# A gated cross-attention and ternary FFN block on one core: weights in column quarters rounded in two steps, TensorE fillers, quantised activations turned by DMA, and new step lists

## The chip, the core and the metric

The kernel runs on one core of a Trainium2 chip. A core has five engines that run their own instruction streams in order: TensorE (PE in the profile, with its weight loads shown apart as PEld), VectorE (DVE), ScalarE (ACT), GpSimd (POOL) and SyncE (SP, which here only issues DMAs). They meet through semaphores. The metric is the device time of one execution in microseconds (us). Three runs of the kernel before took 536.57, 537.95 and 539.39 us; the median is 537.95 us.

## What is computed

The block works on 16 batches of 128 tokens with 512 features. Cut to what matters:

```python
# attention: 32 query heads, 8 key/value heads, head size 16, keys = values = ctx
x = x + tanh(g_xattn) * attention(layernorm(x), ctx, ctx)

# FFN, 512 -> 2048 -> 512
def act_quant(x):                # one scale per token
    s = 127 / clip(max|x|, 1e-5);  return clip(round(x * s), -128, 127) / s
def weight_quant(w):             # one scale per matrix, values -1, 0, 1
    s = clip(mean|w|, 1e-5);       return clip(round(w / s), -1, 1) * s
def h_bitlinear(x, w):
    return act_quant(hadamard(x)) @ weight_quant(w).T
h = silu(h_bitlinear(n, w_gate)) * h_bitlinear(n, w_up)      # n = layernorm(x)
x = x + tanh(g_ffn) * h_bitlinear(h, w_down)
```

## The kernel before, in words

**Steps and lists.** The body is a set of small functions, each a step for one batch `b` (and a part of it). Three lists written out by hand give the order: `PROLOGUE` once, `PLAN` nine times (i = 2 to 10, a step with offset d works on batch i + d), `EPILOGUE` once. `InOrder` (lines 23 to 42) pins each engine's instructions to that order, so the lists are the order of every engine's queue, SP's among them. Every instruction is recorded at line 34, its call; so the profile is read by tile names.

**Attention of one batch.** `normed` takes layer-norm statistics of x (DVE), a power on POOL for 1/sqrt, and applies them (DVE, tile `q`). `q_transposed` turns q on PE (`tpq`), ACT copies it (`qT`). `scores` multiplies with the keys (`sc`, fp32, 32 rows of the array at a time) and DVE takes each row's maximum (`mx`). `split_max` on POOL splits the maxima into three bf16 parts, `max_transposed` turns them (`tpm`, `mT`). `weights` makes the scores the other way round less the maxima (`sT`), ACT takes exp (`ex`); `summed` multiplies with the values (`av`, `avT`); `residual` turns the result back (`tpo`), divides it (DVE, `ga`) and POOL adds it to x.

**FFN of one batch.** `in_norm`: statistics (`stf`, `mvf`, `vef` on DVE, `rstdf` on POOL), DVE applies them (`hn`), POOL does two of the Hadamard steps (`hb`). `in_hadamard` turns that on PE and multiplies with a 128x128 Hadamard matrix (`z`). `in_quant` on DVE: maximum, scale, integers `qe` (int16), and the factors `dq`. `in_transposed` turns qe by four PE transposes (`tpe`) and ACT casts the result to bf16 (`qTe`). `gate_up(b, n)` makes 512 columns of both products (`gu`, bf16, 8 matmuls), `gated` takes Silu on ACT (`sg`) and multiplies on DVE (`h`). `hidden_transposed` turns h (`tpf`, ACT copy `hT`), `hadamard` multiplies (`y`, ACT copy into `za`), `butterfly` does three of the four remaining Hadamard steps on DVE (`zb`, `za`), `magnitudes` takes absolute values on ACT, `out_quant` in three parts finds the maximum (`junk`, `amax_f`) and writes the integers `qf` (int16). `out_transposed` turns each half of qf by eight PE transposes (`tpf<-ident,qf`) and an ACT cast (`qTf`); `out_down` multiplies with w_down (`yo`) and DVE adds x (`res`), which SP sends out.

**Weights, in the prologue.** Each matrix comes as four row quarters of 1 MB (`wst_gate`, `wst_up`, `wst_down`). `mag_*` sums absolute values on ACT, `mean_*` gives the scale. A quarter is then rounded in one of two ways: `rounded_*`, three passes on POOL (multiply and add a large constant, clamp, subtract it), or `compared_*`, two compares on DVE. Two quarters of gate and up go each way; down's four quarters all go to POOL. A row quarter holds all 2048 columns of one chunk of the contraction, so the first `gate_up` needs all four quarters of both matrices.

**Buffers around the change.** Staged weights and the tiles `za` and `zb` share six buffers (`big`). `ps_x` has four PSUM tiles, shared by all transposes and small products, `ps_s` two larger ones for `sc`, `sT` and `gu`. `qf` and `qTf` have one buffer each.

Of the kernel before, what the change touches and what calls it, by code (L numbers as in the profile page):

```python
# [12 lines left out]
I16 = mybir.dt.int16  # L13
AX = mybir.AxisListType
# [4 lines left out]

MAGIC = 12582912.0  # L20
# [25 lines left out]
def flamingo_kernel(  # L46
# [6 lines left out]
    g_attn: bass.AP,  # L53
    g_ffn: bass.AP,
# [3 lines left out]
    h128: bass.AP,  # L58
# [27 lines left out]
    def load_pair(b: int):  # L86
# [14 lines left out]
    load_pair(0)  # L101
    sel_f = w1.tile([P, 2, P], F32, tag="hbT", name="sel_f")
    nc.sync.dma_start(sel_f, sel)
    gates = const.tile([P, 2], F32, name="gates")
    nc.sync.dma_start(gates[:, 0:1], g_attn.partition_broadcast(P))
    nc.sync.dma_start(gates[:, 1:2], g_ffn.partition_broadcast(P))
# [10 lines left out]
    had = const.tile([P, P], F32, name="had")  # L117
    tanh_g = const.tile([P, 2], F32, name="tanh_g")

    wq = {  # L120
        "gate": const.tile([P, KC, FF], BF16, name="wq_gate"),
        "up": const.tile([P, KC, FF], BF16, name="wq_up"),
        "down": const.tile([P, FC, E], BF16, name="wq_down"),
    }
    wsc = const.tile([P, 3], F32, name="wsc")
# [12 lines left out]
    def layer_norm(b: int, kind: str, dst, src):  # L138

        st = tiny.tile([P, 6], F32, tag="st", name=f"st{kind}_{b}")  # L140
        nc.vector.bn_stats(st, xs[b])
        mv = tiny.tile([P, 2], F32, tag="mv", name=f"mv{kind}_{b}")
        nc.vector.bn_aggr(mv, st)
        rstd = tiny.tile([P, 1], F32, tag="rstd", name=f"rstd{kind}_{b}")
        ve = tiny.tile([P, 1], F32, tag="ve", name=f"ve{kind}_{b}")
        nc.vector.tensor_scalar(ve, mv[:, 1:2], EPS, None, ALU.add)
        nc.gpsimd.tensor_tensor(rstd, ve, mhalf, ALU.pow)
        nc.vector.tensor_scalar(dst, src, mv[:, 0:1], rstd, ALU.subtract, ALU.mult)
# [9 lines left out]
    qTs, mTs, exs, avs, maxima = {}, {}, {}, {}, {}  # L158

# [140 lines left out]
    def weight_steps(name: str, src: bass.AP, i: int):  # L300
        NQ = 4
        shape = wq[name].shape
        q = shape[1] // NQ
# [3 lines left out]
        half = const.tile([P, 2], F32, name=f"half_{name}")  # L307
        part = lambda c: wq[name][:, c * q : (c + 1) * q, :]

        def load(c: int):  # L310
            st[c] = big.tile([P, q, shape[2]], F32, tag="big", name=f"wst_{name}_{c}")
            nc.sync.dma_start(
                st[c], src.rearrange("(c p) f -> p c f", p=P)[:, c * q : (c + 1) * q, :]
            )

        def mag(c: int):

            nc.scalar.activation(part(c), st[c], AF.Abs, accum_out=asum[:, c : c + 1])

        def mean():  # L320
            tot = ps_x.tile([P, NQ], F32, tag="x", name=f"tot_{name}")
            nc.tensor.matmul(tot, lhsT=ones, rhs=asum, start=True, stop=True)
            m = tiny.tile([P, 1], F32, tag="mean", name=f"mean_{name}")
            nc.vector.tensor_reduce(m, tot, AX.X, ALU.add)
            nc.vector.tensor_scalar(m, m, 1.0 / NW, EPS, ALU.mult, ALU.max)
            nc.vector.reciprocal(inv, m)
            nc.vector.tensor_scalar(half[:, 0:1], m, 0.5, None, ALU.mult)
            nc.vector.tensor_scalar(half[:, 1:2], m, -0.5, None, ALU.mult)
            nc.vector.tensor_scalar(wsc[:, i : i + 1], m, 1.0 / 127.0, None, ALU.mult)

        def rounded(c: int, k: int):

            s = st[c]
            if k == 0:
                nc.gpsimd.tensor_scalar(s, s, inv, MAGIC, ALU.mult, ALU.add)
            if k == 1:
                nc.gpsimd.tensor_scalar(s, s, MAGIC + 1.0, MAGIC - 1.0, ALU.min, ALU.max)
            if k == 2:
                nc.gpsimd.tensor_scalar(part(c), s, -MAGIC, 1.0, ALU.add, ALU.mult)

        def compared(c: int, k: int):

            if k == 0:
                nc.vector.tensor_scalar(part(c), st[c], half[:, 1:2], None, ALU.is_lt)
            if k == 1:
                nc.vector.scalar_tensor_tensor(
                    part(c), st[c], half[:, 0:1], part(c), ALU.is_gt, ALU.subtract
                )

        return load, mag, mean, rounded, compared  # L350

    load_g, mag_g, mean_g, rounded_g, compared_g = weight_steps("gate", w_gate, 0)
    load_u, mag_u, mean_u, rounded_u, compared_u = weight_steps("up", w_up, 1)
    load_d, mag_d, mean_d, rounded_d, compared_d = weight_steps("down", w_down, 2)

# [6 lines left out]
    def absmax_scale(b: int, name: str, amax, norm: float):  # L362
# [5 lines left out]
        nc.vector.tensor_scalar(a, amax, norm, EPS, ALU.mult, ALU.max)  # L368
        r = tiny.tile([P, 1], F32, tag="r" + name, name=f"r{name}_{b}")
        nc.vector.reciprocal(r, a)  # L370
        nc.vector.tensor_scalar(r, r, 127.0 * norm, None, ALU.mult)
        return a, r

    def transposed16(b: int, name: str, q, qT, c0: int, m: int):

        tp = ps_x.tile([P, m, P], BF16, tag="x", name=f"tp{name}_{b}_{c0}")
        for c in range(m):
            nc.tensor.transpose(
                tp[:, c, :], q[:, (c0 + c) * P : (c0 + c + 1) * P].bitcast(BF16), ident16
            )  # L380
        nc.scalar.copy(qT[:, c0 : c0 + m, :], tp.bitcast(I16))

    hns, zes, ins, hs, hTs, zs, bs, outs, qTs_f = {}, {}, {}, {}, {}, {}, {}, {}, {}

    def in_norm(b: int):
# [4 lines left out]
        for step in (1, 2):  # L390
            dst = w1.tile([P, KC, P], F32, tag=f"hb{step}", name=f"hb{step}_{b}")
# [23 lines left out]
    def in_quant(b: int):  # L415
        z = zes.pop(b).rearrange("p c f -> p (c f)")
        amax = tiny.tile([P, 1], F32, tag="amax_e", name=f"amax_e_{b}")
        nc.vector.tensor_reduce(amax, z, AX.X, ALU.max, apply_absolute_value=True)
        a, r = absmax_scale(b, "e", amax, CE)
        q = w2.tile([P, E], I16, tag="qe", name=f"qe_{b}")  # L420
        nc.vector.tensor_scalar(q, z, r, None, ALU.mult)
        dq = tiny.tile([P, 2], F32, tag="dq", name=f"dq_{b}")
        nc.vector.tensor_scalar(dq, wsc[:, 0:2], a, None, ALU.mult)
        ins[b] = (q, dq)

    def in_transposed(b: int):
        q, dq = ins[b]
        qT = w2.tile([P, KC, P], BF16, tag="qTe", name=f"qTe_{b}")
        transposed16(b, "e", q, qT, 0, KC)
        ins[b] = (qT, dq)  # L430
# [3 lines left out]
    def gate_up(b: int, n: int):  # L434
        qT, _ = ins[b]
        gu = ps_s.tile([P, 2, 512], F32, tag="s", name=f"gu_{b}_{n}")
        for i, w in enumerate(("gate", "up")):
            for c in range(KC):
                nc.tensor.matmul(
                    gu[:, i, :],  # L440
                    lhsT=qT[:, c, :],
                    rhs=wq[w][:, c, n * 512 : (n + 1) * 512],
                    start=(c == 0),
                    stop=(c == KC - 1),
                )
        gus[b, n] = gu

    def gated(b: int, n: int):
        gu, (_, dq) = gus.pop((b, n)), ins[b]
        sg = w2.tile([P, 512], F32, tag="sg", name=f"sg_{b}_{n}")  # L450
        nc.scalar.activation(sg, gu[:, 0, :], AF.Silu, scale=dq[:, 0:1])
        h = w2.tile([P, 512], F32, tag="h", name=f"h_{b}_{n}")
        nc.vector.scalar_tensor_tensor(h, gu[:, 1, :], dq[:, 1:2], sg, ALU.mult, ALU.mult)
        hs[b, n] = h
# [39 lines left out]
    def out_quant(b: int, k: int):  # L494


        if k == 0:
            z, mag = bs[b]
            lo, hi = halves(mag, 8)
            junk = w1.tile([P, FC // 2, P], BF16, tag="junk", name=f"junk_{b}")  # L500
            amax = tiny.tile([P, 1], F32, tag="amax_f", name=f"amax_f_{b}")
            nc.vector.tensor_tensor_reduce(
                out=flat(junk), in0=flat(lo), in1=flat(hi), scale=1.0, scalar=0.0,
# [4 lines left out]
            nc.vector.tensor_scalar(sc, a, wsc[:, 2:3], tanh_g[:, 1:2], ALU.mult, ALU.mult)  # L508
            q = w1.tile([P, FF], I16, tag="qf", name=f"qf_{b}")
# [12 lines left out]
    def out_transposed(b: int, half: int):  # L522
        if half == 0:
            qTs_f[b] = w1.tile([P, FC, P], BF16, tag="qTf", name=f"qTf_{b}")
        transposed16(b, "f", outs[b][0], qTs_f[b], half * 8, 8)
# [3 lines left out]
    def out_down(b: int, half: int):  # L529
# [3 lines left out]
        y, qT = yos[b], qTs_f[b]  # L533
        for c in range(8 * half, 8 * half + 8):
            nc.tensor.matmul(
                y, lhsT=qT[:, c, :], rhs=wq["down"][:, c, :], start=(c == 0), stop=(c == FC - 1)
# [11 lines left out]
    def load_had():  # L548
        nc.sync.dma_start(had, h128)
# [4 lines left out]
    def gates_in():  # L554
# [4 lines left out]
        (load_g, 0),  # L559
        (gates_in,),  # L560
        (load_g, 1),
        (normed, 0),
        (load_g, 2),
        (load_g, 3),
        (q_transposed, 0),
        (fetch, 2),
        (normed, 1),
        (scores, 0, 0),
        (q_transposed, 1),
        (mag_g, 0),  # L570
        (scores, 0, 1),
        (scores, 1, 0),
        (mag_g, 1),
        (split_max, 0),
        (mag_g, 2),
        (normed, 2),
        (values_in, 0),
        (mag_g, 3),
        (mean_g,),
        (scores, 1, 1),  # L580
        (rounded_g, 0, 0),
        (rounded_g, 0, 1),
        (max_transposed, 0),
        (sel_in,),
        (compared_g, 3, 0),
        (rounded_g, 1, 0),
# [472 lines left out]
```

## Time and profile before

| | us |
|---|---|
| median of three runs | 537.95 |
| the profiled execution, whole | 536.77 |
| its span in the profile | 535.0 |
| VectorE busy in the span | 452.5 |
| ScalarE busy | 339.4 |
| GpSimd busy | 217.6 |
| 64 fp32 butterfly halves `zb` on DVE | 84.6 |
| 64 maxima `mx` on DVE | 75.2 |
| 26 ScalarE table loads | 33.4 |
| 12 staged weight quarters: 4 passes of `mag` each for gate, up, down on ACT | 7.6, 7.6, 7.7 |

A row of the groups reads: line, engine, operation, output from input, shape, count | busy us, mean ns of one | idle time of that engine just before, and who ended it. The fp32 matmuls are counted twice (two passes each). A window row gives for a stretch each engine's busy time with the count of instructions, the granted TensorE clock and the DMA share. The profiled execution ended 1.8 us outside its span, and 1.2 us below the median of the runs.

### The profile page before, as it was taken

Reading aid. Unit: us, or ns where it says so; the run is one execution under the profiler, and the core shown is the slowest. Engines: PE = TensorE matmul, PEld = TensorE weight load, DVE = VectorE, ACT = ScalarE, POOL = GpSimd, SP = SyncE. Lnnn points to the kernel's source line nnn. Section 1 sums busy time; section 2 is a strip of 40 time slices with the busy share of each in tenths; the row PEclk is TensorE's granted clock in tenths of the full one; section 3 lists DMA queues with packets and bytes.
Section 4 is the critical chain, followed back from the end, with each engine's and each line's share of the span. In section 5 each row is a group of like instructions: output and inputs, shape, how many; then the busy total and the mean of one; then the engine's idle time right before and its main releaser. Section 6 shows DMA issues by size and latency. Waiting matters only on the chain.

```text
span 535.0 us, 8657 instructions
## 1 busy us (share of the span) xinstructions
PE 480.4 (90%) x3419; PEld 284.6 (53%) x3462; DVE 452.5 (85%) x718; ACT 339.4 (63%) x451; POOL 217.6 (41%) x244
## 2 busy tenths in 40 slices
PE   0887798999899999999999999999999999989946
PEld 0533353655456574646465565656464657567522
DVE  3598985689899989898998998998989898998873
ACT  1637458468757676676758485767758586556641
POOL 2098965979443425252433334342525143030000
PEclk9998569999999999999999999999999999999998
DMA  6927061000000200002000200000000000000001
GB/s 216 399 96 294 17 251 31 1 0 1 1 20 1 90 1 21 1 2 88 2 21 1 89 1 21 1 20 1 21 2 5 17 5 17 20 1 21 20 2 39
DMA packets 12729, 24.88 MB, mean 46 GB/s; under 512 B 1168, under 2 KB 5520, under 8 KB 11664
## 3 DMA queue, kind: packets, MB, share of 16 engines
q1 hardware_dynamic: 12688, 24.32, 12.6%
q8 instruction: 27, 0.44, 0.3%
q14 instruction: 14, 0.11, 0.1%
HBM read 20.12 MB, written 4.19 MB: 45 GB/s over the span
## 4 chain that ended last, share of the span: by engine, by line
PE 39%; DVE 38%; POOL 9%; issue 4%; ACT 3%; POOLq 0%; ACTq 0%
PE gu L34 11%; DVE zb L34 11%; PE y L34 7%; DVE za L34 7%; PE tpf L34 6%; PE sc L34 5%; DVE h L34 4%; PE av L34 3%; PE yo L34 3%; DVE mx L34 2%; DVE qe L34 2%; PE z L34 2%; DVE stf L34 2%; DVE amax_e L34 2%; ACT sg L34 2%
## 5 line engine op out<-in xcount | busy, mean ns | idle before, releaser
L34 DVE TENSOR_TENSOR zb<-za 128x1024 f32<-128x1024 f32 x64 | 84.6, 1363 | 2.9 <-ACT za L34 2.8
L34 DVE TENSOR_REDUCE mx<-sc 128x8 f32<-128x1024 f32 x64 | 75.2, 1216 | 13.9 <-PE sc L34 13.9
L34 PEld LDWEIGHTS <-qTe 128*128 128x128 bf16 x512 | 49.6, 98 | 67.0 <-issue 10.8
L34 ACT ACTIVATE ex<-sT 128x1024 f32<-128x1024 f32 x64 | 62.0, 1021 | 25.7 <-PE sT L34 25.6
L34 PE MATMUL gu<-wq_gate,qTe 128*128 128x512 bf16 x244 | 64.4, 379 | 5.7 <-ACT qTe L34 2.8
L34 POOL TENSOR_TENSOR x<-x,ga 128x256 f32<-128x256 f32 x32 | 34.2, 1073 | 86.4 <-DVE ga L34 86.2
L34 PE MATMUL sc<-kb,qT 32*128 32x256 f32 x512 | 55.6, 458 | 14.1 <-ACT qT L34 6.8
L34 ACT ACTIVATE sg<-gu,dq 128x512 f32<-128x512 f32 x64 | 42.8, 687 | 39.6 <-PE gu L34 36.9
L34 PE MATMUL yo<-wq_down,qTf 128*128 128x512 bf16 x234 | 58.8, 388 | 9.8 <-ACT qTf L34 8.7
L34 PE MATMUL y<-had,hT 128*128 128x128 f32 x512 | 67.6, 277 | 0.0
L34 PE MATMUL gu<-wq_up,qTe 128*128 128x512 bf16 x247 | 63.8, 379 | 0.5
L34 PEld LDWEIGHTS y<-had,hT 128*128 128x128 f32 x512 | 62.1, 192 | 3.6 <-ACT hT L34 3.0
L34 DVE SCALAR_TENSOR_TENSOR h<-gu,dq,sg 128x512 f32<-128x512 f32 x64 | 46.1, 743 | 14.0 <-ACT sg L34 13.9
L34 ACT COPY hT<-tpf 128x512 f32<-128x512 f32 x64 | 37.5, 591 | 30.7 <-PE tpf L34 30.3
L34 PE MATMUL sT<-qT,kb 32*128 32x512 f32 x256 | 49.0, 717 | 5.1 <-DVE mx L34 3.0
L34 PEld LDWEIGHTS sc<-kb,qT 32*128 32x128 f32 x512 | 32.6, 208 | 32.2 <-ACT qT L34 7.2
L34 ACT COPY za<-y 128x512 f32<-128x512 f32 x64 | 37.7, 590 | 15.2 <-PE y L34 15.1
L34 POOL TENSOR_TENSOR hb<-hn 128x256 f32<-128x256 f32 x32 | 41.6, 1319 | 10.6 <-DVE hn L34 10.6
L34 ACT ACT_TABLE_LOAD x26 | 33.4, 1283 | 18.5 <-DMA gates<-in_g_ffn 11.9
L34 PEld LDWEIGHTS <-qTf 128*128 128x128 bf16 x256 | 24.9, 99 | 37.9 <-ACT qTf L34 9.7
L34 DVE TENSOR_TENSOR za<-zb 128x1024 f32<-128x1024 f32 x32 | 44.6, 1436 | 0.1
L34 PE MATMUL tpf<-ident,h 128*128 128x128 f32 x256 | 39.6, 279 | 5.4 <-DVE h L34 5.3
(113 smaller groups left out, 789.4 us busy)
## 6 DMA issues: line engine op xcount, KB each, us to landing
wst_gate<-in_w_gate SPq DMA_DIRECT2D x4, 1024.0 KB, 13.0
wst_up<-in_w_up SPq DMA_DIRECT2D x4, 1024.0 KB, 7.4
wst_down<-in_w_down SPq DMA_DIRECT2D x4, 1024.0 KB, 5.5
out<-res SPq DMA_DIRECT2D x16, 256.0 KB, 2.0
x<-in_x SPq DMA_DIRECT2D x7, 512.0 KB, 6.8
kb<-in_kb SPq DMA_DIRECT2D x8, 256.0 KB, 4.1
kv<-in_kv SPq DMA_DIRECT2D x8, 128.0 KB, 4.0
x<-in_x SPq DMA_DIRECT2D x2, 256.0 KB, 3.4
```

The costliest lines, as they stand in the source:

```text
L34: ins = f(*args, **kwargs)
```

## The change

- **Constants**: the Hadamard matrix and both gates come in one DMA (`aux`) instead of three; `load_had` is gone.
- **Layer norm** is split: `moments_q` and `moments_h` (statistics on DVE; three one-column operations on POOL) and, later in the lists, `normed` and `in_norm`, whose application is now one ACT activation with a per-token scale and bias.
- **Weights** of gate and up come as column quarters (512 columns, all of the contraction), w_down as row quarters as before. Rounding has two passes: `whole` on DVE (scale and min into int32, then max into bf16), for gate and up; `acted` for down (ACT scales into int32, DVE clamps into bf16). Two of up's quarters are staged in w_down's place. POOL rounds nothing any more.
- **Fillers**: `warm(k, 8)`, twelve times in the prologue: eight bf16 128x128x512 matmuls of the identity into an unused PSUM tile.
- **Quantised activations**: `in_quant` keeps maximum and scale on DVE, the integers are written by ACT; `in_transposed` and `out_transposed` send a transposing DMA on SP's queue (part 0) and then an ACT cast in place, SBUF to SBUF (part 1). The 20 PE transposes per batch are gone, and so is `transposed16`.
- **Small operations**: one multiply less in `absmax_scale`; `dq` and `sc` are made on POOL. `qTf` has two buffers; `junk` lies inside `qf`; `hb` of the second step goes back into `hn`.
- **Table loads**: `table(i, k)` loads the exp or Silu tables at a chosen place: two in `PLAN`, six each in `PROLOGUE` and `EPILOGUE`. The built program has 32 loads.
- **Lists**: `gate_up` and `gated` are split in two (gate part, up part); all three lists are new; `PLAN` runs eight times (i = 3 to 10), so the prologue holds one batch step more.

```diff
+    def moments(b: int, kind: str):
         nc.vector.bn_stats(st, xs[b])
         nc.vector.bn_aggr(mv, st)
-        nc.vector.tensor_scalar(ve, mv[:, 1:2], EPS, None, ALU.add)
+        nc.gpsimd.tensor_scalar(ve, mv[:, 1:2], 1.0, EPS, ALU.mult, ALU.add)
         nc.gpsimd.tensor_tensor(rstd, ve, mhalf, ALU.pow)
-        nc.vector.tensor_scalar(dst, src, mv[:, 0:1], rstd, ALU.subtract, ALU.mult)
+        nc.gpsimd.tensor_scalar(nm, mv[:, 0:1], rstd, -1.0, ALU.mult, ALU.mult)
...
+    def layer_norm(b: int, kind: str, dst, src):
+        rstd, nm = norms.pop((kind, b))
+        nc.scalar.activation(dst, src, AF.Identity, scale=rstd, bias=nm)
...
+            if name == "down":
+                nc.sync.dma_start(st[c], rows[:, 4 * c : 4 * c + 4, :])
+            else:
+                nc.sync.dma_start(st[c], rows[:, :, c * 512 : (c + 1) * 512])
...
-        def rounded(c: int, k: int):
...
-        def compared(c: int, k: int):
...
+        def whole(c: int, k: int):
+            w = st[c].bitcast(I32)
+            if k == 0:
+                nc.vector.tensor_scalar(w, st[c], inv, 1.25, ALU.mult, ALU.min)
+            else:
+                nc.vector.tensor_scalar(part[c], w, -1.0, None, ALU.max)
+        def acted(c: int, k: int):
+            w = st[c].bitcast(I32)
+            if k == 0:
+                nc.scalar.activation(w, st[c], AF.Copy, scale=inv)
+            else:
+                nc.vector.tensor_scalar(part[c], w, -1.0, 1.0, ALU.max, ALU.min)
...
+    def warm(k: int, n: int):
+        idle = ps_x.tile([P, 4, P], F32, tag="x", name=f"idle_{k}")
+        for _ in range(n):
+            nc.tensor.matmul(
+                idle, lhsT=ident16, rhs=ident16.unsqueeze(1).to_broadcast([P, 4, P]),
+                start=True, stop=True,
+            )
...
-        nc.vector.tensor_scalar(q, z, r, None, ALU.mult)
-        nc.vector.tensor_scalar(dq, wsc[:, 0:2], a, None, ALU.mult)
+            nc.gpsimd.tensor_scalar(dq, wsc[:, 0:2], a, 1.0, ALU.mult, ALU.mult)
+            nc.scalar.activation(q, z, AF.Copy, scale=r)
...
-        transposed16(b, "e", q, qT, 0, KC)
+            nc.sync.dma_start(qT, q, transpose=True)
+            nc.scalar.copy(q.bitcast(BF16), q)
...
-        transposed16(b, "f", outs[b][0], qTs_f[b], half * 8, 8)
+            nc.sync.dma_start(qT, outs[b][0][:, half * FF // 2 : (half + 1) * FF // 2], transpose=True)
+            nc.scalar.copy(qT.bitcast(BF16), qT)
...
+    def table(i: int, k: int):
+        nc.scalar.preload_act_table((AF.Exp, AF.Silu)[k])
...
-    for i in range(2, 11):
+    for i in range(3, 11):
```

The new `PLAN`, the first third of its 62 steps, in which the DMA transposes lie (part 0 is the DMA, part 1 the ACT cast):

```python
(hadamard, -1, 2), (out_quant, -2, 2), (in_hadamard, 0, 1), (max_transposed, 2),
(in_quant, 0, 0), (residual, 1, 0), (in_quant, 0, 1), (butterfly, -1, 1), (weights, 2, 0),
(out_transposed, -2, 1, 0), (out_transposed, -2, 1, 1), (in_transposed, 0, 0),
(moments_h, 1), (in_transposed, 0, 1), (butterfly, -1, 2), (out_down, -2, 0),
(q_transposed, 3), (weights, 2, 1), (out_down, -2, 1), (gate_up, 0, 0, 0), ...
```

The first half of `qf` goes at the end of the list, `(out_transposed, -1, 0, 0)`, with its cast five steps later as the last step.

## The prediction

> **What bounds the kernel now.** I read the busy table, then the chain of waits for a repeating piece, the windows of one repetition, and last the timelines of the start and the end.
>
> ```profile
> PE 480.4 (90%) x3419; PEld 284.6 (53%) x3462; DVE 452.5 (85%) x718; ACT 339.4 (63%) x451; POOL 217.6 (41%) x244
> ...
> 140.05 2.26 DVE zb L34 x2
> ...
> 169.08 2.26 DVE zb L34 x2
> ...
> 198.11 2.26 DVE zb L34 x2
> ...
> 236.90:265.90 29.00, 28.07 (x214) 16.91 (x216) 26.18 (x44) 20.08 (x28) 10.72 (x14) 1.00 0.13 42
> ```
>
> The chain repeats every 29.02 us: one pass through `PLAN`. The window row (columns PE, PEld, DVE, ACT, POOL) shows PE busy 28.07 of 29.00, DVE 26.18, ACT 20.08. So the steady part is PE's; its 0.93 us of idle are mostly waits of 0.38 and 0.28 us for `h`. DVE is close behind. The butterfly of 140.05 stands 4.8 us behind the top of the list, so nine passes run from 135.2 to 396.4, after a prologue of 135.2 us and before an epilogue of 138.6.
>
> Two stages differ. In the prologue the array runs at half speed:
>
> ```profile
> 29.87 3.21 PE L34 MATMUL sT<-qT,kb 32*128 32x512 f32 x8 [0.56 <-DVE mx L34]
> 255.17 1.14 PE L34 MATMUL sT<-qT,kb 32*128 32x512 f32 x8
> ...
> 32.71 3.01 POOL L34 TENSOR_SCALAR wst_gate<-wst_gate,inv_gate 128x2048 f32<-128x2048 f32 x1
> 37.78 2.91 DVE L34 TENSOR_SCALAR wq_gate<-wst_gate,half_gate 128x2048 bf16<-128x2048 f32 x1
> 32.68 1.28 DVE L34 TENSOR_SCALAR wq_gate<-wst_gate,half_gate 128x2048 bf16<-128x2048 f32 x1
> ```
>
> The same eight matmuls take 3.21 us early and 1.14 us later. The same DVE compare takes 1.28 or 2.91 us, as POOL's rounding runs beside it. And at the end PE has little to do: busy 11.48 us of the last 24.
>
> **The change, part by part.**
>
> *Transposes.* In the steady windows PE's 20 bf16 transposes of a batch are these rows:
>
> ```profile
> L34 PE MATMUL tpf<-ident,qf 128*128 128x128 bf16 x256 | 19.3, 222 | 0.5 <-DVE unused L34 0.5
> L34 PE MATMUL tpe<-ident,qe 128*128 128x128 bf16 x64 | 6.3, 221 | 1.8 <-DVE qe L34 1.8
> ...
> out<-res SPq DMA_DIRECT2D x16, 256.0 KB, 2.0
> x<-in_x SPq DMA_DIRECT2D x7, 512.0 KB, 6.8
> kb<-in_kb SPq DMA_DIRECT2D x8, 256.0 KB, 4.1
> kv<-in_kv SPq DMA_DIRECT2D x8, 128.0 KB, 4.0
> x<-in_x SPq DMA_DIRECT2D x2, 256.0 KB, 3.4
> ```
>
> (19.3 + 6.3) / 16 = 1.60 us of PE per batch go. PE needs 26.47; with the same 0.93 idle the period is 27.40. Three DMAs come instead: 256 KB per half of `qf`, 128 KB for `qe`. No transposing DMA is in the trace. The nearest rows are plain DMAs, 2.0 to 4.0 us to landing; I take 3.4 for a half, that is 2.0 fixed and 0.175 us for each of its eight 128x128 blocks. Two rules of the Trainium skill disagree: *VectorE: DVE Perf Modes*, "The three transpose paths", gives 1309 ns to a 128x128 block by DMA against 390 ns on TensorE, and says to use TensorE where PSUM will do: it speaks against this change. At that price per block, in series, a batch would take 20 x 1.309 = 26.2 us of the queue. *Advanced Engine Details and Errata*, "X-Bar Transpose (TRN2)", calls transposing DMAs as fast as regular ones. 1309 ns for a lone block is less than the 2.0 us of this trace's quickest DMA, so I read it as mostly fixed cost and stay with the rows; both ends are kept.
>
> Is the landing hidden? Count from the top of the new `PLAN`. `out_quant(-2, 2)` is DVE's first step (1.28), so the second half goes out at about 1.5. Behind it on SP waits `in_transposed(0, 0)`: its integers are ready after `z`, the maximum (0.69), two small operations and the ACT pass, near 3.7. With b us per block the activations land at 1.5 + 12b + 2.0, with b = 0.175 at 5.6. Needed: PE has `hadamard` 0.92, `z` 0.91, `tpm` 0.30, two `weights` 1.60 each, two halves of `yo` 1.73 each and `tpq` 0.47 before `gate_up`, so 9.3; behind the cast on ACT still stand itself (0.6), `qT` (0.6) and an exp of 1.0 whose PSUM buffer `gate_up` takes, so 7.2. Cover 1.6 us; it is gone at b = 0.31. ACT blocks for whatever lands late, and the exps behind it. SP's output and fetch stand behind both DMAs and nobody waits for them soon; the first half goes out a third of a period ahead of its cast.
>
> *VectorE to ScalarE.* DVE loses per batch `q` 0.56, `hn` 0.55, `qe` 0.75, four small ones of 0.154, `dq` 0.32, `sc` 0.26: 3.05 us, and the waits for POOL's power, (12.1 + 10.7) / 16 = 1.43. DVE stands at 23.1: no bound. ACT gains a pass for each big one. The nearest row is `sg<-gu,dq`, 687 ns with one per-token operand; at 0.7 to 0.8 for three passes ACT goes from 20.08 to about 22.3 of 27.4, hidden beside PE. The casts keep their size (1027 and 595 ns) and change only their source. Statistics now stand well ahead of their use, so POOL's three small operations (0.55 for the power, some 0.2 each else, and as much for `dq` and `sc`) are hidden in its 16 idle us. Table loads: two a period before and after, 1.28 each; nothing gained.
>
> *Weights.* POOL's 57 us and DVE's 23.4 of compares (6.2 + 4.2 + 7.5 + 5.5) become 20 DVE passes and 4 on ACT (1.93 each, by `wq_down<-wst_down`). A DVE pass costs between 1.28 and 2.9 by the two rows above; POOL no longer fights, so 1.28: 26 us, hardly more than before. With 2.9 it would be 32 us worse on an engine that has 25 to 30 to spare. Column quarters let the first `gate_up` start after one rounded quarter of each matrix. DMA in 2 KB rows instead of 8 KB: the DMAs were busy 0.53 of the first 90 us and PE and DVE had work of the first batches beside them, so nothing; `aux` for three small DMAs, a fraction of 1 us.
>
> *Fillers.* PE was busy 65.70 us up to 90.15. The steps listed there (9 `scores`, 8 `weights`, 6 `summed`, 6 `residual` and so on) come to 38 us at steady prices (1.13, 1.60, 1.03, 0.49): some 27 us are slow clock. The skill's *TensorE: Matmul & The Clock Gate*, Part 1, explains half speed until some 3.4 us of sustained work, but puts the ramp below 1% of a kernel, 5 us here; the rows make it 27, for PE kept falling back. (The granted clock in the window of 20 to 40 us reads 1.00 while durations are double; I believe the durations.) Twelve fillers of 8 cost 12 x 8 x 0.216 = 20.7 us warm. The first two lie in the first 14 us, where PE idles 12.8. Of the other ten, 17.3 us, I put half in idle that exists: 8.6 net.
>
> *The prologue's sum.* The new one ends about one period later: 135.2 + 29.0 = 164.2, but counting steps it holds two `scores`, two `weights`, two `summed` and a few transposes less, 8 us, which the epilogue gets. 164.2 - 8 - 27 - 2.5 (transposes) + 8.6 = 135; DVE free of POOL should save some of the 11.7 us of PE idle between 14 and 90, I take 3: **132**.
>
> *The epilogue.* By list prices PE has 119.5 us of work against 119.8, but 1.7 more ahead of the last butterflies. At the end:
>
> ```profile
> 524.23 1.28 DVE L34 CUSTOM_DVE_ANT_0 qf<-zb,rf 128x1024 int16<-128x1024 f32 x1
> 525.38 1.49 PE L34 MATMUL tpf<-ident,qf 128*128 128x128 bf16 x16
> 526.52 1.93 ACT L34 CAST qTf<-tpf 128x1024 bf16<-128x1024 int16 x2 [4.58 <-PE tpf L34]
> 527.59 3.63 PE L34 MATMUL yo<-wq_down,qTf 128*128 128x512 bf16 x16 [0.71 <-ACT qTf L34]
> ```
>
> Here a DMA of 3.4 takes the place of 0.9 us on PE, with nothing beside it: +2.5. 138.6 + 1.7 + 2.5 = **142.8**.
>
> *Sum.* 132 + 8 x 27.4 (219.2) + 142.8 = 494.0 us of span. The profiled execution had 1.8 outside it: 495.8 against 536.8, 41 less. The median of the runs stands 1.2 above the profiled one: 497.
>
> **Rivals.**
>
> *Better: the handovers close too.* DVE and ACT no longer press on PE, four PSUM tiles serve fewer users, fillers lie wholly in idle. Period 26.7, prologue 124 (114.8 of PE with fillers, and a start of 9), epilogue 139.5: 213.6 + 124 + 139.5 + 1.8, with the 1.2, is **480**. For it: PE idle of 12.8 early is real. Against: PE was 97% busy, and ACT gets fuller.
>
> *Part is given back.* b of 0.42 makes each batch 1.4 us late, or the fillers don't hold the clock and half of the 27 us stays. Period 28.8 (230), prologue 139, epilogue 147: with 3.0, **519**. For it: landing rows up to 4.0, and ACT's order without slack behind the cast.
>
> *Slower: the crossbar works block by block.* Place: SP's queue, the second half of `qf` and `qe` in series at the top of each period. It decides when it costs the 41 us over some 15 batches, 2.7 each: b = 0.31 + 2.7 / 12 = 0.54 us a block. With 1.309 the activations land at 19.2, 12 us late: over 15 batches 180, so **677**. For it: the page's figure. Against: plain rows at 0.175, a third of the point.
>
> *The change doesn't do what it says*: the loads placed by hand come on top. The built program has 32 against 26; 6 x 1.28 = 7.7 us of ACT, in stages where ACT has 20 us and more to spare, so the forecast stands. Fillers too few to keep the clock are in the second rival.
>
> **How the numbers follow.** Forecast 497: 0.56. Better 480: 0.20. Given back 519: 0.16. Slower or equal: 0.08, of which 0.02 within 0.5% (about what runs of this kernel can tell from no change). Faster by more than that: 0.92. The range goes from 478, just under the better case, to 521, just over the one given back; beyond it lie the fourth case and tails of the other three, some 0.16.
>
> **What would show it.** A period of 27 to 27.8 between repeated butterflies with PE about 26.5 busy; transposing DMAs landing within 4 us and no wait of PE for `qTe`; `sT` of the first batches at 1.2 us, not 3.2; first `whole` passes near 1.3; DVE near 23 and ACT near 22 a period. Wrong, if ACT's casts wait for DMA by over 1 us a period, if DVE passes stay near 2.9, or if early matmuls still take double.

## The result, and the profile after

| | before | after |
|---|---|---|
| median, 11 runs each | 536.57 | 532.26 |
| all runs | 534.01 to 539.39 | 530.43 to 534.95 |
| profiled execution, its span | 536.77, 535.0 | 530.72, 528.9 |

The ratio is 0.9925, with a 95% interval of 0.9896 to 0.9953: a gain of 4.3 us, clear of the noise but under 1%, where 41 had been forecast; 532 lies outside the range. The busy table and the window of one pass in the steady part, from one first butterfly to the next (columns PE, PEld, DVE, ACT, POOL):

```profile
PE 457.0 (86%) x3205; PEld 263.2 (50%) x3238; DVE 401.7 (76%) x580; ACT 388.8 (74%) x509; POOL 220.9 (42%) x316
...
206.93:235.60 28.67, 26.23 (x198) 15.48 (x196) 23.34 (x36) 22.38 (x31) 13.85 (x19) 1.00 0.15 33
```

The busy times are those of the forecast (26.47, 23.1, 22.3). What is not is the first number: the pass takes 28.67, so PE stands idle for 2.44 us of it instead of 0.93. Work was taken from PE, and the pass got only 0.33 us shorter. The waits of PE say for whom it stands:

```profile
PE gu L33 <- ACT sg L33: 30.8, 30, 2.5
PE yo L33 <- ACT qTf L33: 14.1, 5, 10.8
PE tpm L33 <- POOL m_pad L33: 5.3, 12, 1.0
```

(us in total, times, longest.) The first row is new. `gu` is written by PE and `sg` is the Silu that reads it, so PE waits, before it writes, for a reader of what it wrote earlier. The timelines of PE and of ACT in one pass show the case:

```profile
214.50 1.03 PE L33 MATMUL gu<-wq_gate,qTe 128*128 128x512 bf16 x4
216.36 1.02 PE L33 MATMUL gu<-wq_up,qTe 128*128 128x512 bf16 x4 [0.84 <-ACT sg L33]
...
226.11 1.02 PE L33 MATMUL gu<-wq_up,qTe 128*128 128x512 bf16 x4 [1.26 <-ACT sg L33]
```

```profile
215.62 0.69 ACT L33 ACTIVATE sg<-gu,dq 128x512 f32<-128x512 f32 x1 [0.15 <-PE gu L33]
...
225.37 0.69 ACT L33 ACTIVATE sg<-gu,dq 128x512 f32<-128x512 f32 x1
```

The Silu ends at 216.31 and 226.06, and 0.05 us later the up half starts. It needs nothing from the Silu. But `gate_up` now comes in two halves, both halves still go into one PSUM tile `gu`, and the list has `gated(b, n, 0)`, the Silu that reads the first half, between them. If dependences are kept by tile, a write to the second half waits for the read of the first: a false wait, twice a pass, 2.1 us. The first three experiments test that. The rest of what was forecast for a row is there:

```profile
23.69 1.14 PE L33 MATMUL sT<-qT,kb 32*128 32x512 f32 x8
...
L33 DVE TENSOR_SCALAR wst_gate<-wst_gate,inv_gate 128x2048 int32<-128x2048 f32 x4 | 5.1, 1294 | 0.1
L33 DVE TENSOR_SCALAR wq_gate<-wst_gate 128x2048 bf16<-128x2048 int32 x4 | 4.9, 1214 | 0.0
...
qTf<-qf SPq DMA_TRANSPOSE x32, 3.1
qTe<-qe SPq DMA_TRANSPOSE x16, 2.4
```

The first batch's `sT` takes 1.14 us (3.21 before), the rounding passes of gate 1.2 to 1.3 us, and the transposing DMAs land after 3.1 and 2.4 us (last column, median).

### The profile page after: what moved, and what is told of

It is laid out like the page before. It is cut to its first block, busy times and chain, and to the rows that moved or that the text cites. A ratio compares the mean times of both kernels' runs of the same rounds, so it can differ in the third digit from the quotient of the medians.

```text
span 528.9 us, 8306 instructions
## 1 busy us (share of the span) xinstructions
PE 457.0 (86%) x3205; PEld 263.2 (50%) x3238; DVE 401.7 (76%) x580; ACT 388.8 (74%) x509; POOL 220.9 (42%) x316
## 2 busy tenths in 40 slices
DMA packets 58007, 35.33 MB, mean 67 GB/s; under 512 B 43376, under 2 KB 47728, under 8 KB 57968
## 4 chain that ended last, share of the span: by engine, by line
PE 56%; ACT 15%; DVE 12%; POOL 8%; issue 4%; DMA 4%; SPq 1%; ACTq 0%; DVEq 0%; POOLq 0%
PE gu L33 16%; PE yo L33 8%; DVE mx L33 7%; PE sT L33 6%; PE y L33 6%; PE sc L33 6%; ACT sg L33 4%; PE tpf L33 4%; POOL m_pad L33 3%; ACT za L33 3%; PE av L33 3%; ACT ex L33 2%; PE tpo L33 2%; DVE zb L33 2%; DMA qTf<-qf 1%
## 5 line engine op out<-in xcount | busy, mean ns | idle before, releaser
L33 PE MATMUL gu<-wq_up,qTe 128*128 128x512 bf16 x253 | 64.3, 378 | 30.9 <-ACT sg L33 30.8
L33 DVE TENSOR_TENSOR zb<-za 128x1024 f32<-128x1024 f32 x64 | 81.2, 1310 | 3.7 <-ACT za L33 3.6
L33 PE MATMUL y<-aux,hT 128*128 128x128 f32 x512 | 66.2, 277 | 0.1
L33 PEld LDWEIGHTS y<-aux,hT 128*128 128x128 f32 x512 | 62.5, 192 | 5.3 <-issue 2.0
L33 POOL TENSOR_TENSOR x<-x,ga 128x256 f32<-128x256 f32 x32 | 43.3, 1355 | 48.8 <-DVE ga L33 46.9
L33 POOL TENSOR_TENSOR hb<-hn 128x256 f32<-128x256 f32 x32 | 25.6, 821 | 44.4 <-ACT hn L33 44.4
L33 ACT ACT_TABLE_LOAD x32 | 41.1, 1283 | 3.2 <-PE gu L33 1.9
L33 POOL CAST m_pad<-mx 128x32 bf16<-128x32 f32 x16 | 5.4, 336 | 88.5 <-DVE mx L33 88.5
L33 PE MATMUL sT<-qT,kb 32*128 32x512 f32 x256 | 40.7, 640 | 1.8 <-ACT ex L33 1.8
L33 PE MATMUL sc<-kb,qT 32*128 32x256 f32 x512 | 39.0, 401 | 3.2 <-ACT qT L33 2.5
L33 DVE CUSTOM_DVE_ANT_0 qf<-zb,rf 128x1024 int16<-128x1024 f32 x32 | 41.1, 1288 | 0.5
L33 ACT CAST qTf<-qTf 128x1024 bf16<-128x1024 int16 x32 | 33.5, 1046 | 7.7 <-DMA qTf<-qf 7.5
## 6 DMA issues: line engine op xcount, KB each, us to landing
wq_down<-in_w_up SPq DMA_DIRECT2D x2, 1024.0 KB, 13.5
```

The lines of the kernel that those rows point to most:

```text
L33: ins = f(*args, **kwargs)
```

## Experiments

"Own PSUM" below is the kernel of experiment 2. Times are medians; before had 535.6 to 536.8 beside them. Stages are counted from the start of the first butterfly of a pass, less 3.7 us to the top of the list, each from one profiled execution. In runs with the same list such a stage differs by up to 2.8 us (ahead of the passes 141.7 in experiment 2 and 139.9 in experiment 8; behind them 145.3 in experiment 2 and 148.1 in experiment 6 without fillers), so less than that says nothing.

**1. The wait alone taken away, by order.** In the lists the Silu step now comes behind the up half:

```diff
...
         (gate_up, 0, 1, 0),
         (table, 0, 1),
         (gated, 0, 0, 0),
+        (gate_up, 0, 1, 1),
         (gated, 0, 1, 0),
         (normed, 4),
         (butterfly, -1, 4),
-        (gate_up, 0, 1, 1),
...
```

> Only the lists differ: every Silu step gated(b, n, 0) now stands behind gate_up(b, n, 1), so the up half no longer waits for the Silu that reads the other half of the same PSUM tile. In PLAN no engine's own order changes, only the wait goes; at the two ends about a dozen steps move past one to three others. Theory A (the wait of the up half for the Silu is the new bound): the wait of 2.1 us a pass goes, the period falls from 28.67 to 26.6 to 27.2 with PE idle below 1 us, and with the waits at the ends the kernel takes 503 to 510 us. Rival B (the wait only shows where PE waits for DVE and POOL anyway, by the chain mx, m_pad, tpm or by h): another wait takes its place, period 28.3 or more, 525 to 533 us.

512.55 us, ratio 0.9551 (0.9521 to 0.9581). The row `PE gu <- ACT sg` is gone from PE's waits. One pass:

```profile
202.62:229.56 26.94, 26.84 (x198) 16.05 (x196) 23.18 (x35) 22.44 (x31) 14.90 (x19) 1.00 0.16 35
```

No instruction of the pass changed its place on its engine, and the period fell by 1.73. Theory A's period came; the total is 2.5 us above its range. PE is idle for only 0.10 us, yet part of the wait is still there, counted as busy. It sits in `scores`. The same step in the changed kernel, then here:

```profile
218.31 1.15 PE L33 MATMUL sc<-kb,qT 32*128 32x256 f32 x16
...
212.81 1.83 PE L33 MATMUL sc<-kb,qT 32*128 32x256 f32 x16
213.51 0.73 PEld L33 LDWEIGHTS sc<-kb,qT 32*128 32x128 f32 x12 [0.40 <-DVE h L33]
```

A row of PE runs from its first matmul to its last, and here the loads of twelve of the sixteen stand until `h` is done. `sc` and `gu` share the two large PSUM tiles, and `h` is the last reader of `gu`. It comes later because the shared tile still ties the halves, the other way round: the Silu starts at 211.99, when the up half is done (211.89), though the gate half was ready at 211.03. A pass has 0.98 us more in `sc` (3.27 against 2.29 in the changed kernel), the whole kernel 10.4 (49.4 against 39.0).

**2. The wait alone taken away, by buffers ("own PSUM").** The lists stay as they are:

```diff
-            gus[b, n] = ps_s.tile([P, 2, 512], F32, tag="s", name=f"gu_{b}_{n}")
+            gus[b, n] = [ps_s.tile([P, 512], F32, tag="s", name=f"gg_{b}_{n}"), None]
+        else:
+            gus[b, n][1] = ps_x.tile([P, 512], F32, tag="x", name=f"gup_{b}_{n}")
...
```

> The lists are those of the changed kernel. The gate half and the up half get a PSUM tile each (one of the two large ones, one of the four small ones) instead of sharing one, so the Silu keeps its early place and the up half has nothing to wait for. Theory A: period 26.6 to 27.2, 500 to 510 us, as in the reordered one. If the reordered one is fast and this one is not, the small PSUM tiles have become short: waits of PE for their readers, period 28 or more. Rival B: 525 us or more in both.

497.40 us, ratio 0.9256 (0.923 to 0.9283): 34.9 us less than the changed kernel, and below both kernels of the case.

```profile
197.88:224.12 26.24, 25.90 (x198) 15.50 (x196) 23.23 (x35) 22.15 (x31) 13.82 (x19) 1.00 0.16 36
```

PE is busy 25.90 of 26.24. Against order, the Silu keeps its early place, and `sc` takes 2.29 us a pass and 39.5 in all: that is 9.9 of the 12.4 us of span between the two runs. Rival B falls with both: with order a smaller wait took the place of the false one (0.98 us for 2.1), here none did.

**3. The same wait put into the kernel before.** There the Silu comes after both halves. Here it is written between them, in the same tile:

```diff
                 )
+            if i == 0:
+                sg = w2.tile([P, 512], F32, tag="sg", name=f"sg_{b}_{n}")
+                nc.scalar.activation(sg, gu[:, 0, :], AF.Silu, scale=ins[b][1][:, 0:1])
-        gus[b, n] = gu
+        gus[b, n] = (gu, sg)
```

> The kernel before, where the Silu of the gate half is written between the gate matmuls and the up matmuls of the same PSUM tile; PE's order is unchanged. Theory A: every up half waits about 1.0 us for its Silu (the changed kernel's 30 waits were 30.8 us), four a batch: 60 us less what PE had idle beside it, 575 to 600. Rival B (PE is early and waits anyway elsewhere): 536 to 545.

610.92 us, ratio 1.1397 (1.1344 to 1.1451), 74 us more: above the range of A, far from B. PE's first row of waits:

```profile
PE gu L34 <- ACT sg L34: 70.4, 64, 2.4
```

64 blocks, 64 waits, 1.1 us each. The expectation took idle time of PE off the sum; the time grew by no less than the waits, so little or none of them fell into idle time.

**4. Turns by TensorE again, in the changed kernel and with own PSUM.** DMA part 0 becomes eight (or four) PE transposes into a `ps_x` tile, part 1 the cast from it:

```diff
...
-            nc.sync.dma_start(qT, outs[b][0][:, half * FF // 2 : (half + 1) * FF // 2], transpose=True)
+            tps[b, half] = turned(f"f_{b}_{half}", outs[b][0][:, half * FF // 2 : (half + 1) * FF // 2], 8)
```

> The changed kernel with the quantised activations turned on TensorE again (20 bf16 transposes a batch into PSUM, casts from PSUM), all lists as they are. If the transfers are hidden, as the steady trace shows, and PE sets the pace: 1.6 us a batch more on PE, less 2.5 at the end, 553 to 558 us, period 30.2. Rival C (the DMA turns hold something back that the trace doesn't put down to them, such as SP's queue or ACT's order): 532 or less.

> Own PSUM tiles for the gate and up halves, and the quantised activations turned on TensorE again. With the wait for the Silu gone PE is busy 25.90 of 26.24 us a pass, so nothing is left to hide the 20 transposes: if my price of 1.60 us a batch is right, the period is 27.8 and the kernel takes 515 to 522 us (497.4 + 16 x 1.6, less up to 4 at the end). Rival (the turns are cheap on PE, and the DMA buys mostly free PSUM tiles): below 510.

548.82 and 513.94 us: 16.6 and 16.5 more than with DMA, not 25. With own PSUM the pass is

```profile
199.84:226.75 26.91, 26.80 (x222) 16.59 (x216) 23.18 (x35) 22.31 (x31) 13.84 (x19) 1.00 0.03 10
```

so 20 transposes cost 0.67 us of period (26.91 less 26.24; in the changed kernel also 0.67, 29.34 less 28.67), where their rows say 1.60. With own PSUM the span grew by 15.2: 0.3 ahead of the passes, 5.4 in them, 9.4 behind. Some 3 us of the last lie behind the last butterfly (20.1 us are left there, 16.8 with DMA). The list may be the cause: written for DMA, it has the last batch's turns ahead of batch 14's `yo`, and PE stands 12.4 us at them. Another list was not tried.

**5. Turns by DMA alone, in the kernel before.** Issued where the integers are made, cast at the old places:

```diff
...
+            nc.sync.dma_start(
+                qTs_f[b][:, 8 * h : 8 * h + 8, :], q[:, h * FF // 2 : (h + 1) * FF // 2], transpose=True
+            )
...
-        transposed16(b, "f", outs[b][0], qTs_f[b], half * 8, 8)
+        nc.scalar.copy(qT.bitcast(BF16), qT)
```

> The kernel before with one part of the change alone: the quantised activations are turned by DMA (issued where they are quantised, cast on ACT at the old place), lists unchanged. By the rows of TensorE's transposes (1.60 us a batch, as predicted): 511 to 515 us. By what the turns cost in the two pairs of runs so far (0.67 us a pass, the rest at the end only): 525 to 531. If the landing is late for the unchanged lists: 536 or more, with ACT waits for qTf or qTe.

555.06 us, ratio 1.0342 (1.0294 to 1.0389): slower. The third of the expected cases, larger than thought. Two rows of its waits:

```profile
ACT qTf L34 <- DMA qTf<-qf: 22.8, 16, 7.0
...
PE gu L34 <- ACT qTe L34: 10.4, 3, 5.0
```

In a list where the cast stands close behind the quantisation, ACT waits 1.4 us a batch for the landing, on the mean. The period is 29.6 instead of 29.0, which is 5 us in the nine passes; the span grew by 18.4, so the ends lose 13. The transfer is no slower here (3.0 us to landing for a half): it is the new lists that hide it in the changed kernel.

**6. Fillers.** Without any in the changed kernel; without any, and with the first four groups (7, 5, 11, 9), with own PSUM; and twelve groups put into the first 65 us of the kernel before:

```diff
-        (warm, 7, 8),
...
-        (warm, 5, 8),
...
-        (warm, 6, 8),
```

> The changed kernel without its 12 groups of 8 filler matmuls. My prediction's price: the slow clock costs 27 us, fillers 8.6 net, so without them the kernel is 18 us slower: 550, with sT of the first batches at 3.2 us again. Rival: the fillers cost about what they bring, or a denser prologue keeps the clock by itself: 528 to 536 us, sT partly at 1.2.

> Own PSUM tiles, no fillers at all. In the changed kernel all fillers together were worth 3.3 us. The same here: 499 to 502. By my prediction's price (27 us of slow clock against 8.6 net): 515. If early fillers are what counts, this one is 5 or more above the one with the first four groups.

> Own PSUM tiles, and only the first four groups of fillers (7, 5, 11, 9, up to some 24 us) are kept. The other eight are 15.2 us of PE where PE is 85 to 95% busy. If the clock holds without them: 486 to 492 us. If it falls back as in the changed kernel without fillers (slow rows at 43 and 94 us), the two cancel: 494 to 500. If they carry the clock through the whole prologue: above 500.

> The kernel before with 12 groups of 8 fillers in its first 65 us, nothing else. By my prediction (27 us of slow clock gone, 8.6 paid): 518. By the runs without fillers (3 us): 532 to 536. If they push work back in a prologue whose VectorE is held up by POOL: 540 or more.

535.55 us against 532.26 with them; 500.32 (none) and 499.82 (four) against 497.40; 536.91 against 536.76 for before. Twelve groups are worth 3.3 us in the changed kernel and nothing in the old lists. With own PSUM the ranges overlap (497.9 to 505.2 for none, 498.5 to 501.1 for four, 496.7 to 499.6 for all, four runs each), so which groups count is not settled. The slow rows do come back without them:

```profile
24.61 2.09 PE L33 MATMUL sT<-qT,kb 32*128 32x512 f32 x8
28.23 2.14 PE L33 MATMUL sT<-qT,kb 32*128 32x512 f32 x6
...
94.62 2.14 PE L33 MATMUL sT<-qT,kb 32*128 32x512 f32 x6 [1.58 <-ACT ex L33]
```

To see how much that is, take each of PE's rows up to the top of the first pass (before: one pass further, to 164.2) and subtract its count times the busy time of one in a steady pass. What is left over is 32 us before, 24 in the changed kernel without fillers, and 9 with them, beside 26.7 for the fillers themselves. So they recover 15 and cost 27. PE is then busy 125.0 us of 145.9 with them and 115.4 of 149.8 without: 9.6 more busy, 13.5 less idle, 3.9 gained. In the kernel before twelve groups recover 18 for 25.8 and gain nothing.

What is left over is not all slow clock, for a wait inside a row counts too. The eight `sT` of 3.21 us before take 2.09 above; before, the second four had their weights loaded only after a wait:

```profile
31.00 0.50 PEld L34 LDWEIGHTS sT<-qT,kb 32*128 32x128 f32 x4 [0.62 <-DVE mx L34]
```

**7. Small operations back from POOL to VectorE**, with own PSUM: variance plus epsilon, `dq` and `sc`.

```diff
-        nc.gpsimd.tensor_scalar(ve, mv[:, 1:2], 1.0, EPS, ALU.mult, ALU.add)
+        nc.vector.tensor_scalar(ve, mv[:, 1:2], 1.0, EPS, ALU.mult, ALU.add)
...
```

> Own PSUM tiles, and three of the one-column operations (variance plus epsilon, dq, sc) go back from POOL to VectorE, where one takes 0.15 to 0.3 us; POOL's rows for them read 0.3 to 0.9 us. Theory: in the passes PE sets the pace and hides both, period 26.2 as without it; at the two ends the POOL chain of layer norm shortens by 0.5 to 1 us a batch: 493 to 496 us. Rival: POOL's rows are long because they are counted over waits for VectorE's butterflies, and VectorE's queue delays them as much: 497 to 499. If VectorE becomes late by them: 500 or more.

498.77 us (498.02 to 500.90) against 497.40 (496.72 to 499.61): no gain. Eight passes took 212.3 us instead of 210.8. The first pass began 1.8 us earlier, but so it did in experiment 8, whose prologue is that of experiment 2, so this is the spread of executions. POOL's rows of 0.86 (`vef`) and 0.91 us (`sc`) looked dear, and moving them bought nothing.

**8. The last batch alone turned by TensorE**, with own PSUM, and batch 14's `out_down` moved ahead of the last butterfly:

```diff
+        (out_transposed, 14, 0, 1),
+        (out_down, 14, 0),
+        (out_down, 14, 1),
         (butterfly, 15, 4),
...
```

> Own PSUM tiles for the halves, and for the last batch alone the two halves are turned on TensorE at the place of their cast; the down projection of batch 14 moves ahead of the last butterfly. My prediction priced the transfer at the very end at 2.5 us: 494 to 495.5 by that. If PE's slow clock after its idle eats it: 497.

502.98 us: slower than without, and the fault is in the edit. From its timeline:

```profile
476.06 5.60 PE L33 MATMUL yo<-wq_down,qTf 128*128 128x512 bf16 x16 [5.10 <-ACT qTf L33]
481.76 0.75 DVE L33 SCALAR_TENSOR_TENSOR res<-yo,sc,x 128x512 f32<-128x512 f32 x1 [5.38 <-issue]
482.42 2.35 DVE L33 TENSOR_TENSOR zb<-za 128x1024 f32<-128x1024 f32 x2
```

`out_down(14, 1)` also issues `res` on DVE, which now stands ahead of the butterfly and waits 5.38 us for `yo`. Behind that butterfly 15.6 us are left (500.4 less 484.8), against 16.8 with DMA (497.8 less 481.0). That is 1.2 us for the turn at the end, from single profiles and with a list that differs there, so a hint only.

## Why the prediction was wrong

| stage, us of span | predicted | changed | own PSUM |
|---|---|---|---|
| up to the first pass of `PLAN` | 132 | 145.9 | 141.7 |
| eight passes | 219.2 | 230.0 | 210.8 |
| after them | 142.8 | 153.0 | 145.3 |
| sum | 494.0 | 528.9 | 497.8 |

**The step that failed: "with the same 0.93 idle the period is 27.40".** PE's busy time had been worked out and its idle time taken over. The change splits `gate_up` and `gated` and writes one between the halves of the other. That part stood in the change and was given no price at all; the buffer of the first `gate_up` was looked at, that of the up half was not. In its place the runs show 2.1 us a pass of false wait, and 14 us of it at the two ends (30.8 in all). Taking it away brought 34.9 us in the medians and 31.1 between the two profiled spans: 19.2 in the passes, 4.2 ahead of them, 7.7 behind. The rival "part is given back" named the period, 28.8, for other reasons: a late landing, or a clock not held. In the steady pass of the changed kernel no wait of PE is put down to a landing. The better rival gave 26.7 to a period without handovers; without the false wait it is 26.24.

Taking over 0.93 of idle was wrong the other way too. Before, that idle was waits for `h`, and 0.75 us a pass of the same kind lay inside the rows of `sc` (3.04 us a pass, 2.29 in the new lists), counted as busy. With own PSUM PE is idle 0.34 and busy 25.90, not 26.47.

**That own PSUM lands on 497, the forecast, is luck.** Its stages miss in both directions: 9.7 too long ahead of the passes, 8.4 too short in them, 2.5 too long behind (the last within the spread of executions).

**Transposes: mechanism right, size wrong.** 1.60 us a batch, their rows' busy time, is 0.67 of period. Rows of PE overlap: with own PSUM those of a pass add up to 30.3 us in a busy time of 25.90, so the busy time of a row is more than its removal gives back. PE came to 25.90 although the turns gave less: beside `sc`, other rows that the change does not touch shrank (`tpf<-ident,h` from 2.5 to 2.3 a pass, `y` 4.3 to 4.1, `yo` 3.9 to 3.7). That the new lists pack them closer is likely, and was not tried by itself.

**The landing: right.** A half was forecast to land after 3.4 us and took 3.1. The activations were to land 5.6 us behind the top of the list and to be needed at 7.2: their DMA is issued at 207.05 in the pass shown, 3.8 behind the top, and lands 2.4 later (the median), at 6.2; the cast starts at 7.1 and did not wait. No matmul waits for `qTe` in a steady pass. The slower rival is dead as a price per block: at 1309 ns a half would take 10.5 us. Its place was well chosen all the same, for in the old lists (experiment 5) the same transfers make the kernel slower. That the transfer fits is a property of the list.

**VectorE to ScalarE: right.** 23.34 and 22.38 us a pass. **Table loads: right in size**, 32 take 41.1 us where 26 took 33.4. In the pass shown the Silu behind the first load still waits 0.19 us for PE, so that load costs nothing; at the ends this was not looked at.

**Weights: right in size.** In the seven forms of rounding passes up to 110 us the mean is between 1214 and 1528 ns. One reading was wrong: the compare of 2.91 us was put down to POOL's rounding beside it, but the compare of 1.28 us had POOL beside it as well, in the row of 3.01 us that the prediction shows. The short one began at 32.68, just ahead of that row (32.71). The long one began at 37.78, inside this row, which lasts to 39.61:

```profile
35.69 3.92 POOL L34 TENSOR_SCALAR wq_gate<-wst_gate 128x2048 bf16<-128x2048 f32 x1
```

In this pair the later to start was the longer; the last section has the same for POOL.

**Fillers: the term mis-sized.** Forecast was 27 us gone for 8.6 paid, 18.4 net; measured are 3.3. The 27 was a fair count of the excess in PE's busy time (32 by the rows), but part of that is waits inside the rows, and all of it was priced as if it lay on the path. Recovered were 15, at 26.7 of filler instead of 20.7, in part because fillers ran slow themselves (the first 16 took 6.14 us). *TensorE: Matmul & The Clock Gate*, Part 1, in the Trainium skill puts the ramp below 1% of a kernel, 5 us here. The prediction set it aside for the rows. For busy time the rows are right; that what could be got back, 3 us, lies near the page's figure is chance, since PE's rows are slow again and again and not at the start alone (24.61, 28.23 and 94.62 us without fillers). The term is 15.1 us too large, more than the 9.7 by which the stage ahead of the passes was missed with own PSUM.

**Small POOL operations**: 0.2 us each assumed, 0.3 to 0.9 in the rows on the mean, and no gain from moving three of them (experiment 7). **The end**: +2.5 forecast; from the last butterflies on, 24.0 us after and 23.1 before, +0.9.

## What to carry to other kernels

When a change splits a step, follow each half to the buffer that it writes and ask who reads the other half in between: one tile shared by two halves ties the writer of one to the reader of the other, and the trace shows it as an engine waiting for the consumer of its own product. A row of matmuls that grows without more work in it hides a wait, and busy time counts it. Price an instruction taken from a pipelined engine by what its neighbours gain, which here was 0.67 us where its rows said 1.60, and price time run at a slow clock by the idle time around it. Test a forecast by stages: a total that fits may be the sum of three misses.

## What the runs showed of the hardware that was not expected

- **Handing a PSUM tile from ACT's read back to PE takes 0.05 us in the trace** (216.31 to 216.36). The dear part of such a wait is the reader's 0.69 us and its place in ACT's queue, not the handing over.
- **PE is slow after an idle stretch of 5 to 11 us at the end**: 16 matmuls of `yo` take 5.60 us after 5.10 idle (experiment 8) and 5.96 after 10.80 (own PSUM, granted clock 0.72 over the last 24 us), and 15 of them 3.63 right behind.
- **POOL's one-column rows are long when VectorE is in a large pass**: `rstdf` reads 1204 ns on the mean after and 552 before. It has two lengths. Eleven of the 16 start inside a butterfly or rounding pass of VectorE and take 1.41 to 2.36 us; the other five take 0.55 to 0.57. Before, all 16 start while VectorE does none, and take 0.55 to 0.58. One of the long ones, and the pass beside it:

```profile
211.88 1.41 POOL L33 TENSOR_TENSOR rstdf<-vef,mhalf 128x1 f32<-128x1 f32 x1
...
210.55 2.33 DVE L33 TENSOR_TENSOR za<-zb 128x1024 f32<-128x1024 f32 x2
```

  The butterfly keeps its 1.2 us a half. The Trainium skill, *Perfetto Trace Analysis*, "GPSIMD Engine Instruction", calls a GpSimd instruction's span in a profile unreliable and says to time it by the spacing of starts. Here the spacing agrees with the span: the next instruction, `nmf`, starts 1.51 us after a long `rstdf` and 0.65 after a short one.
- **Transposing DMAs are many small packets**: 43376 of 58007 packets under 512 bytes (1168 of 12729 before), and yet 3.1 us for eight blocks of 128x128 with two-byte elements.
